# Cross-attention block with adaptive layer norms: half a score tile lowered by VectorE straight out of PSUM, two of four normalisations on GpSimd, one of four statistics on ScalarE, and a new order of the calls

## The chip, the core and the metric

The kernel runs on one core of one Trainium2 chip. The metric is the device time of one execution in microseconds (us), the median of several runs. One core has five engines that work side by side, each through its own queue of instructions in order: TensorE (PE in the profile; PEld is its weight load), VectorE (DVE), ScalarE (ACT), GpSimd (POOL) and SyncE (SP), which issues nearly all DMAs here.

## The reference

Everything is float32. There are 16 batches of 1024 query rows of 512 features, a context of 64 rows per batch, and 16 heads of 32 features.

```python
def _ada_ln(x, c, W_ss, b_ss):
    mu = jnp.mean(x, axis=-1, keepdims=True)
    var = jnp.mean((x - mu) ** 2, axis=-1, keepdims=True)
    h = (x - mu) / jnp.sqrt(var + EPS)
    ss = jax.nn.silu(c) @ W_ss + b_ss
    scale, bias = jnp.split(ss, 2, axis=-1)
    return (1.0 + scale)[:, None, :] * h + bias[:, None, :]
...
xq = _ada_ln(x_q, t_vec, Wss_q, bss_q)
xkv = _ada_ln(x_kv, t_vec, Wss_kv, bss_kv)
q = (xq @ Wq + bq).reshape(B, Lq, nh, dh)
kv = (xkv @ Wkv + bkv).reshape(B, Lkv, 2, nh, dh)
...
scores = jnp.einsum('bqhd,bkhd->bhqk', q, k) / jnp.sqrt(jnp.float32(dh))
attn = jax.nn.softmax(scores, axis=-1)
out = jnp.einsum('bhqk,bkhd->bqhd', attn, v).reshape(B, Lq, H)
return x_q + (out @ Wp + bp)
```

## The kernel before

The queries are cut into 32 blocks of 512 rows, numbered 0 to 31. The prologue computes the modulation, the keys K and the values V of all batches and starts the first blocks; a loop `for i in range(3, NB - 2)` (i from 3 to 29) is the steady state; a written-out tail finishes blocks 30 (`y`) and 31 (`z`). The steps of one block are spread over several turns of the loop, so that a turn works on six blocks at once: i, the two before it (`a = i - 1`, `b = i - 2`) and the ones after it.

The order of the instructions on every engine is the order in which the program calls the steps; no scheduler moves them. The tile framework adds the waits: an instruction waits for the last writer of what it reads, for the last readers of what it overwrites, and, where a PSUM tile is read by two engines, the later reader in program order waits for the earlier one.

The steps of one block that matter here, with the lines of the kernel before:

- `q_stats` (L286, L287): mean and variance of a block's rows, four parts t = 0 to 3 of 128 rows, on VectorE (BN_STATS and BN_AGGR). `q_scale` (L295 to L304) turns them into a scale and a shift on ScalarE and GpSimd. `hidden` (L327) normalises a part in place on ScalarE.
- `turn` (L357) transposes 32 by 32 on VectorE, `move` (L382) finishes the transposition with 16 DMAs, `scale_features` (L442) applies the modulation on ScalarE.
- The product with Wq is a seven-product scheme (Strassen): `query_product` n = 2 to 6, with the first and the seventh product split again by the same scheme into 4 and 3 quarter products (`quarter_products`, L605). GpSimd makes the sums of the operands (`feature_sums` L493, `feature_quarters` L581 to L583); ScalarE and VectorE read the results out of PSUM (`query_out`, `query_added`, `quarter_copies`, `quarter_adds`).
- `score_products(i, z)` (L738), z = 0 and 1 for the two halves of the 64 context rows: 16 small products that fill two PSUM tiles, `ps_i_z_0` and `ps_i_z_1` (half e = 0 and e = 1 of the score tile). There are only two such buffers (`ps_s`, `bufs=2`), shared by both halves z and by the result of `mix`. So `score_products(i, 1)` waits until both tiles of z = 0 have been read, and `mix` until both tiles of z = 1 have been.
- `maximum(i, z, e)` (L755) takes the column maxima of a PSUM tile on VectorE; `copied(i, z, e)` (L764) copies it to SBUF on ScalarE. Both read the same tile. `maxima` (L775, L784) joins the maxima of both halves and spreads them over a tile `mb`; `subtract` (L797) takes `mb` from each score half on GpSimd, in place in SBUF; `weights` (L808) is the exponential on ScalarE; `total` (L858) adds both halves on GpSimd, `row_total` (L863) sums the columns on VectorE, `inverse_rows` (L878) inverts them.
- `mix` (L936) multiplies by V, `divided` (L915) divides by the sums while it reads PSUM.
- The product with Wp is again a seven-product scheme, `product(i, n)` (L1086), with operand sums `row_sum` on GpSimd (L1051 to L1058). Its products accumulate in two PSUM banks, and `added(i, n)` (L1116) adds a finished product to the residual on VectorE.

In the loop before, each score half is read crosswise: VectorE begins with tile e = 0 while ScalarE copies e = 1, and then they change over.

## Time and profile before

| | |
|---|---|
| time, median of 3 runs | 997.28 us (996.85 to 998.1) |
| span of the profiled execution | 996.9 us |
| TensorE busy | 984.2 us (99%) |
| VectorE busy | 895.6 us (90%) |
| GpSimd busy | 895.4 us (90%) |
| ScalarE busy | 779.3 us (78%) |
| one turn of the loop (500.00 to 528.52) | 28.52 us |

The span runs from the first to the last instruction of the profiled execution; the median is 0.4 us above it. Busy times are sums of the records of an engine over the span. The end of a matmul's record is modelled, so TensorE is better read from the starts of its records. In the views below a row of the timeline holds start, duration, engine, line, operation, output<-input, number of records, and in brackets the idle time ahead of it and what ended it. Each float32 matmul of the program shows as two records.

### The profile page before, as it was taken

The page shows a single profiled execution, that of the slowest core. Times are in us where ns is not written, and L with a number is a line of the kernel's source. Part 1 is how long each engine was busy: PE and PEld are TensorE (multiplying, and loading weights), DVE is VectorE, ACT ScalarE, POOL GpSimd, SP SyncE. Part 2 cuts the span into 40 slices and gives each one's busy share as a digit, 9 for nine tenths or more (in the row PEclk, how much of TensorE's full clock was granted, in tenths as well). Part 3 has the DMA queues.
Part 4 walks back from the last instruction along what each step waited for, and adds up shares of the span by engine and source line. Part 5 has one row for each costly group of instructions (what it writes and reads, how often), then busy time and mean ns, then how long its engine had stood idle before and what let it go on. Part 6 is the DMA issues. An engine that isn't in the chain of part 4 may idle for free.

```text
span 996.9 us, 20564 instructions
## 1 busy us (share of the span) xinstructions
PE 984.2 (99%) x7465; PEld 760.7 (76%) x7465; DVE 895.6 (90%) x1318; ACT 779.3 (78%) x1165; POOL 895.4 (90%) x690
## 2 busy tenths in 40 slices
PE   7999999999999999999999999999999999999998
PEld 6878777787777877877778778777787787777756
DVE  7696899999999999999999999999999999987786
ACT  3878878888888888888888888888888888876620
POOL 2677899999999999999999999999999999999681
PEclk9999999999999999999999999999999999999999
DMA  9765655555655555566655555665555555544422
GB/s 308 264 165 151 156 164 156 140 165 180 190 181 176 159 165 152 151 182 186 183 176 152 173 145 155 185 188 178 176 150 175 151 154 182 148 132 130 145 85 97
DMA packets 115188, 165.77 MB, mean 166 GB/s; under 512 B 34920, under 2 KB 46464, under 8 KB 113168
## 3 DMA queue, kind: packets, MB, share of 16 engines
q1 hardware_dynamic: 114704, 163.93, 55.2%
q8 instruction: 59, 0.97, 0.4%
q0 software_dynamic: 384, 0.54, 0.2%
q14 instruction: 41, 0.34, 0.1%
HBM read 79.47 MB, written 34.60 MB: 114 GB/s over the span
## 4 chain that ended last, share of the span: by engine, by line
PE 88%; DMA 4%; DVE 3%; SPq 2%; POOL 1%; issue 1%; ACT 0%; DVEq 0%; POOLq 0%
PE pp L1086 36%; PE pq L534 27%; PE pq L605 10%; PE ps L738 6%; PE po L936 5%; PE pk_A L534 1%; PE pk_B L534 1%; DMA w_k_sb<-in_L_xcond_Wkv_dram 1%; DMA r<-in_x_dram 1%; PE pv_B L534 1%; DMA ltd<-lt 1%; DMA V_B<-stage_B 1%; DMA vr<-ltd 0%; POOL sum L858 0%; DVE l L826 0%
## 5 line engine op out<-in xcount | busy, mean ns | idle before, releaser
L797 POOL TENSOR_TENSOR s<-s,mb 128x2048 f32<-128x2048 f32 x64 | 290.6, 4564 | 20.3 <-DVE mb L784 13.4
L1086 PE MATMUL pp<-w_p_sb,ot 128*128 128x256 f32 x740 | 174.8, 379 | 1.1 <-DVE ot L915 1.1
L764 ACT COPY s<-ps 128x1024 f32<-128x1024 f32 x128 | 129.3, 1013 | 46.1 <-PE ps L738 34.0
L755 DVE TRANSPOSE_TENSOR_REDUCE m<-ps 128x32 f32<-128x1024 f32 x128 | 152.4, 1228 | 10.4 <-PE ps L738 9.3
L1086 PEld LDWEIGHTS pp<-w_p_sb,ot 128*128 128x128 f32 x740 | 138.2, 190 | 20.5 <-issue 2.8
L645 ACT ACTIVATE qt<-pq,bias_t 128x256 f32<-128x256 f32 x256 | 107.8, 475 | 48.8 <-PE pq L605 27.7
L858 POOL TENSOR_TENSOR sum<-s,p 128x2048 f32<-128x2048 f32 x30 | 136.5, 4549 | 1.6 <-ACT p L808 1.6
L1116 DVE TENSOR_TENSOR r<-pp,r 128x512 f32<-128x512 f32 x183 | 120.3, 669 | 13.8 <-ACT xt L442 6.8
L534 PE MATMUL pq<-xt,w_q_sums 128*128 128x256 f32 x512 | 123.8, 385 | 0.0
L534 PEld LDWEIGHTS pq<-xt,w_q_sums 128*128 128x128 f32 x512 | 95.0, 190 | 34.6 <-issue 22.6
L1086 PE MATMUL pp<-WT,ot 128*128 128x256 f32 x492 | 118.4, 383 | 0.0
L1086 PE MATMUL pp<-WT,s 128*128 128x256 f32 x488 | 116.1, 380 | 1.3 <-DVE r L1107 0.8
L817 ACT ACTIVATE s<-s 32x2048 f32<-32x2048 f32 x60 | 114.6, 1910 | 1.8 <-DMA p<-s 0.4
L1086 PEld LDWEIGHTS pp<-WT,ot 128*128 128x128 f32 x492 | 90.9, 190 | 19.1 <-issue 4.2
L1086 PEld LDWEIGHTS pp<-WT,s 128*128 128x128 f32 x488 | 88.2, 190 | 13.1 <-POOL s L1056 1.3
L327 ACT ACTIVATE x<-x,rstdq 128x512 f32<-128x512 f32 x128 | 94.8, 807 | 1.0 <-POOL rstdq L304 1.0
L442 ACT ACTIVATE xt<-xt,ss_q 128x512 f32<-128x512 f32 x124 | 94.0, 809 | 1.0 <-DMA xt<-ht 0.7
L915 DVE TENSOR_TENSOR ot<-po,vb 128x1024 f32<-128x1024 f32 x62 | 73.0, 1219 | 17.6 <-PE po L936 17.4
L286 DVE BATCH_NORM_STATS2 bs<-x 128x6 f32<-128x512 f32 x128 | 85.3, 666 | 0.0
L493 POOL TENSOR_TENSOR xt_sums<-xt 128x512 f32<-128x512 f32 x64 | 81.2, 1269 | 2.0 <-DMA x<-in_x_dram 1.3
L357 DVE STREAM_TRANSPOSE ht<-x 128x512 f32<-128x512 f32 x124 | 77.7, 679 | 4.7 <-DMA xt<-ht 2.2
L891 DVE STREAM_TRANSPOSE vb<-vr 128x2048 f32<-128x2048 f32 (+1 forms) x33 | 73.7, 2236 | 4.4 <-DMA vr<-ltd 4.4
(224 smaller groups left out, 1963.8 us busy)
## 6 DMA issues: line engine op xcount, KB each, us to landing
x<-in_x_dram SPq DMA_DIRECT2D x32, 1024.0 KB, 5.3
r<-in_x_dram SPq DMA_DIRECT2D x32, 1024.0 KB, 5.9
xt<-ht SPq DMA_DIRECT2D x488, 64.0 KB, 2.0
out_dram<-r SPq DMA_DIRECT2D x60, 512.0 KB, 4.7
p<-s SPq DMA_DIRECT2D x60, 256.0 KB, 3.8
wss_kv<-in_L_xcond_Wss_kv_dram SPq DMA_DIRECT2D x4, 512.0 KB, 7.2
wss_q<-in_L_xcond_Wss_q_dram SPq DMA_DIRECT2D x4, 512.0 KB, 11.0
vr<-ltd SPq DMA_DIRECT2D x128, 8.0 KB, 1.7
```

The lines of the kernel that those rows point to most:

```text
L327: nc.scalar.activation(dst, src, AF.Identity, bias=rstd[:, 1, j : j + 1], scale=rstd[:, 0, j : j + 1])
L442: nc.scalar.activation(xt[:, :, c, :], xt[:, :, c, :], AF.Identity, scale=ss["q"][:, c, b : b + 1], bias=ss["q"][:, NC + c, b : b + 1],)
L534: nc.tensor.matmul(out_, lhsT=lhsT, rhs=rhs, start=new and m == 0 and c == 0, stop=c == HC - 1, skip_group_check=True,)
L605: nc.tensor.matmul(qa["q", k][:, q * P : (q + 1) * P], lhsT=lhsT, rhs=rhs, start=first and q == 0, stop=True, skip_group_check=True,)
L645: nc.scalar.activation(dst, src, AF.Identity, bias=bq_t[:, o : o + 1])
L755: nc.vector.tensor_reduce(m_tiles[i][:, z, 2 * e : 2 * e + 2, :], s_banks[i, z][e].rearrange("p r (j a) -> p r j a", a=32), AX.X, ALU.max, ...
L764: nc.scalar.copy(s_tiles[i, z][:, 2 * e : 2 * e + 2, :], s_banks[i, z][e])
L797: eng.tensor_tensor(s_tiles[i, z], s_tiles[i, z], mb_tiles[i], ALU.subtract)
L817: nc.scalar.activation(s_tiles[i, 0][at + 32 : at + 64], raw_tiles[i][at : at + 32], AF.Exp, scale=SCALE)
L858: nc.gpsimd.tensor_tensor(t, s_tiles[i, 0], s_tiles[i, 1], ALU.add)
L1086: nc.tensor.matmul(to, lhsT=rows[:, c, t * P : (t + 1) * P], rhs=cols[:, c, :], start=n == 2 and (i, 2) not in seeded and t == 0 and c == ...
L1116: nc.vector.tensor_add(r, a, r)
```

## The change

In the loop:

- `copied(i, 1, 0)` (ScalarE) is gone. A new step `lowered(i, 0)` on VectorE reads the PSUM tile of z = 1, e = 0, subtracts `mb` and writes SBUF. The other half of z = 1 is still copied by ScalarE, and GpSimd subtracts on that half alone (`subtract_half`).
- Parts t = 0 and 1 of a block are normalised on GpSimd (`hidden_apart`), parts 2 and 3 as before on ScalarE.
- The statistics of part t = 0 are made on ScalarE (`q_stats_two`: two activations with a running sum, then a small GpSimd operation); parts 1 to 3 as before on VectorE.
- All calls of the prologue and of the loop stand in a new order. The loop's body is cut elsewhere: its first part, under `if i >= 4`, finishes the work of the turn before, and a written-out copy of it follows the loop. In the new order a turn begins `score_products(i, 0)`, `product(b, 6)`, `copied(i, 0, 0)`, `maximum(i, 0, 0)`, `maximum(i, 0, 1)`, `product(b, 7)`, the first quarter products, `copied(i, 0, 1)`, `added(b, 6)`, `score_products(i, 1)`.
- The small pools hold fewer buffers (`m2` 2 for 3, `lt` and `vr` 1 for 2). The tail after the loop is the same code, but for the part of Wp that is loaded again, which is now 512 KB instead of 256 KB.

Several new functions (`inner_*`, `exchanged`, `weights_whole`, `reciprocal_rows`, `read_rows`) are defined and never called.

```diff
+    def q_stats_two(i, ts, last=False):
...
+        for t in ts:
+            x = x_tiles[i][:, t, :]
+            junk = rpool.tile([P, HPC * TB], F32, tag="spread", name=f"squares_{i}_{t}")[:, :H]
+            nc.scalar.activation(junk, x, AF.Identity, scale=1.0 / H, accum_out=mv[:, t, 0:1])
+            nc.scalar.activation(
+                junk, x, AF.Square, scale=-1.0, bias=mv[:, t, 0:1], accum_out=mv[:, t, 1:2]
+            )
...
+    def hidden_apart(i, t):
+
+        row, rstd = x_tiles[i][:, t, :], q_rstd[i]
+        nc.gpsimd.tensor_scalar(
+            row, row, rstd[:, 0, t : t + 1], rstd[:, 1, t : t + 1], ALU.mult, ALU.add
+        )
...
+    def lowered(i, e):
+        rs = slice(2 * e, 2 * e + 2)
+        nc.vector.tensor_tensor(
+            s_tiles[i, 1][:, rs, :], s_banks[i, 1][e], mb_tiles[i][:, rs, :], ALU.subtract
+        )
+
+    def subtract_half(i, z, e):
+        rs = slice(2 * e, 2 * e + 2)
+        s = s_tiles[i, z][:, rs, :]
+        nc.gpsimd.tensor_tensor(s, s, mb_tiles[i][:, rs, :], ALU.subtract)
...
         score_products(i, 0)
...
+        product(b, 6)
...
+        copied(i, 0, 0)
...
         maximum(i, 0, 0)
...
+        maximum(i, 0, 1)
...
         quarter_products(n, 1, True)
-        product(b, 6)
         copied(i, 0, 1)
...
-        maximum(i, 0, 1)
         quarter_copies(n, 1)
-        copied(i, 0, 0)
...
```

The order is shown at three places, all at the beginning of the turn i = 15, in rows of operation, output<-inputs and size. `pq` is a query product, `pp` an output product, `ps_15_z_e` a score tile, `r` the residual, `lt` the row totals, `m2` the maxima.

TensorE before, ahead of `score_products(15, 0)`: query product 4, output product 2 of block 13, query product 3, output product 7, then the scores.

```order
L534 MATMUL pq_15_7_4623<-xt_sums_517,w_q_sb_101 128x256 x4
L1086 MATMUL pp_13_2_4711<-w_p_sb_104,ot_13_4686 128x256 x4
L534 MATMUL pq_15_1_4553<-xt_15_4192,w_q_sums_401 128x256 x4
L1086 MATMUL pp_13_3_4760<-WT_1338,ot_13_4686 128x256 x4
L738 MATMUL ps_15_0_0_4802<-qt_15_4614,K_A_130 32x512 x2
```

The same place on TensorE after the change.

```order
L1159 MATMUL pp_13_2_4690<-w_p_sb_104,ot_13_4688 128x256 x4
L558 MATMUL pq_15_1_4571<-xt_15_4219,w_q_sums_404 128x256 x4
L558 MATMUL pq_15_7_4647<-xt_sums_492,w_q_sb_101 128x256 x4
L1159 MATMUL pp_13_2_4734<-w_p_sb_104,ot_13_4688 128x256 x4
L762 MATMUL ps_15_0_0_4766<-qt_15_4644,K_A_130 32x512 x2
```

Output product 2 (`pp_13_2_4711` before, `pp_13_2_4734` after) has moved from three groups ahead of the scores to right in front of them, and output product 7 from ahead of the scores to between the two score halves.

VectorE before, around the maxima of the first score half.

```order
L1116 TENSOR_TENSOR r_13_4523<-pp_13_2_4711,r_13_4523 128x2x256
L652 TENSOR_TENSOR qt_15_4614<-pq_15_7_4623,qt_15_4614 128x2x4x32 x2
L863 TENSOR_REDUCE lt_14_4779<-sum_14_4722 128x64
L878 RECIPROCAL lt_14_4779<-lt_14_4779 128x64
L755 TENSOR_REDUCE m2_15_4820<-ps_15_0_0_4802 128x32
L755 TENSOR_REDUCE m2_15_4820<-ps_15_0_1_4803 128x32
```

The same place on VectorE after the change.

```order
L1292 TENSOR_TENSOR r_13_4471<-pp_13_2_4734,r_13_4471 128x2x256
L914 TENSOR_REDUCE lt_14_4803<-sum_14_4728 128x64
L779 TENSOR_REDUCE m2_15_4784<-ps_15_0_0_4766 128x32
L779 TENSOR_REDUCE m2_15_4784<-ps_15_0_1_4767 128x32
L929 RECIPROCAL lt_14_4803<-lt_14_4803 128x64
```

The row totals stand now directly between the addition of output product 2 and the two maxima.

ScalarE before, the copies of the first score half.

```order
L764 COPY s_15_0_4821<-ps_15_0_1_4803 128x1024
L616 COPY t_quarters_129<-pq_16_1_4823 128x256
L764 COPY s_15_0_4821<-ps_15_0_0_4802 128x1024
L817 ACTIVATE s_14_0_4551<-s_14_1_4584 32x2048
L546 COPY pq_16_2_4866<-pq_16_1_4823 128x512
```

The same place on ScalarE after the change.

```order
L788 COPY s_15_0_4785<-ps_15_0_0_4766 128x1024
L1104 COPY pp_13_3_4806<-b_diff_134 128x512
L296 ACTIVATE workq_4810<-mvq_18_4730,eps_sb_114 128x4
L297 ACTIVATE workq_4810<-workq_4810,ln_half_116 128x4
L299 ACTIVATE workq_4810<-workq_4810 128x4
L300 ACTIVATE workq_4810<-mvq_18_4730,eps_sb_114 128x4
L301 ACTIVATE workq_4810<-mvq_18_4730 128x4
L788 COPY s_15_0_4785<-ps_15_0_1_4767 128x1024
L640 COPY t_quarters_129<-pq_16_1_4842 128x256
```

Before, the copy of e = 1 comes first and waits for TensorE alone, and the copy of e = 0 waits for the maximum of e = 0. After, the copy of e = 0 comes first, both maxima follow on VectorE, and the copy of e = 1 waits for VectorE's maximum of e = 1.

More of the change, by code (lines that the diff above doesn't have):

```diff
@@ new lines, in cross_attention_block @@
+    q_scale(3)
+    context_product('B', 'k', 7)
+    query_out(1, 2)
+    move(2, ks=(0,))
+    move(2, ks=(1,))
+    query_product(1, 6)
+    copied(0, 1, 0)
+    hidden(3, (0,))
+    maximum(0, 1, 1)
+    hidden(3, (1,))
+    hidden(3, (3,))
+    query_out(1, 6)
+    load_x(4)
+    context_product('B', 'k', 6)
+    maximum(0, 1, 0)
+    move(2, ks=(2,))
+    query_product(1, 7)
+    context_out('B', 'k', 6)
+    query_product(1, 5)
+    maxima(0)
+    q_stats(4, (0,))
+    context_out('B', 'k', 7)
@@ new lines, in cross_attention_block @@
+    product(0, 2)
+    weights(1, 0)
+    query_out(2, 3)
+    query_added(2, 4)
+    nc.gpsimd.tensor_tensor(b_diff, b_second, b_first, ALU.subtract)
+    value_move('B', (1,))
+    score_products(2, 0)
+    hidden(4, (3,))
+    q_stats(5, (3,))
+    product(0, 1)
+    copied(2, 0, 1)
+    value_move('B', (3,))
+    turn(4, (1,))
+    turn(4, (2,))
+    copied(2, 0, 0)
+    turn(4, (3,))
+    total(1)
+    maximum(2, 0, 0)
+    maximum(2, 0, 1)
+    row_total(1)
+    query_product(3, 1)
+    load_x(6)
@@ L1505, in cross_attention_block @@
+    move(4, ks=(3,))
+    again(1, 1)
     weight_sums()
[L1506 to L1509 removed]
     maximum(2, 1, 0)
     maxima(2)
+    subtract(2, zs=(0,))
+    product(0, 6)
+    added(0, 6)
+    hidden(5, (3,))
     product(0, 7)
[L1513 to L1518 removed]
+    product(0, 5)
+    q_stats(6, (0,))
+    copied(2, 1, 0)
     added(0, 7)
     product(0, 4)
[L1521 removed]
@@ new lines, in cross_attention_block @@
+        if i >= 4:
+            hidden(f, (3,))
+        if i >= 4:
+            query_seed(i)
+        if i >= 4:
+            added(i - 3, 5)
+        if i >= 4:
+            product(i - 3, 4)
+        if i >= 4:
+            maxima(a)
+        if i >= 30:
+            load_residual(NB - 1)
+        if i >= 4:
+            query_product(i, 2)
+        if i >= 4:
+            again(b, 1)
+        if i >= 4:
+            turn(f, (0,))
+        if i >= 4:
+            copied(a, 1, 1)
+        if i >= 4:
+            lowered(a, 0)
@@ new lines, in cross_attention_block @@
+        if i >= 4:
+            turn(f, (3,))
+        if i >= 4:
+            total(a)
+        if i >= 4 and i <= 28:
+            q_stats_two(i + 3, (0,))
+        if i >= 4:
+            output_seed(b)
+        if i >= 4:
+            query_out(i, 3)
+        if i >= 4 and i <= 28:
+            q_stats(i + 3, (1,))
+        if i >= 4:
+            row_sum(b, 1)
+        if i >= 4:
+            load_residual(a)
+        if i >= 4:
+            product(b, 2)
+        if i >= 4 and i <= 28:
+            q_stats(i + 3, (2,))
@@ L1705, in cross_attention_block @@
-    y, z = NB - 2, NB - 1
+    product(27, 5)
+    quarter_products(30, 1, False)
+    maximum(29, 1, 1)
+    maximum(29, 1, 0)
+    feature_quarters(30, 7)
+    query_seed(30)
+    added(27, 5)
+    product(27, 4)
+    maxima(29)
+    load_residual(NB - 1)
+    query_product(30, 2)
+    again(28, 1)
+    copied(29, 1, 1)
+    lowered(29, 0)
+    product(27, 3)
+    query_out(30, 2)
+    quarter_products(30, 7, True)
+    quarter_copies(30, 7)
+    query_product(30, 6)
+    scale_features(31, (1,))
```

1106 lines of the change are left out of this document (623 added, 483 removed).

## The prediction

> **What bounds the kernel now.** I read the page first, then the chain of waits, then one turn of the loop stretch by stretch. The page's first part:
>
> ```profile
> PE 984.2 (99%) x7465; PEld 760.7 (76%) x7465; DVE 895.6 (90%) x1318; ACT 779.3 (78%) x1165; POOL 895.4 (90%) x690
> ```
>
> TensorE is busy in 99% of the span, but its ends are modelled, so the starts have to show whether it really never waits. The chain of the end, in order of time, gives the same piece of every turn:
>
> ```profile
> 501.22 3.45 PE pq L534 x16
> 505.56 3.46 PE pp L1086 x16
> 529.74 3.45 PE pq L534 x16
> ```
>
> One turn takes 529.74 - 501.22 = 28.52 us, and 16 records of 128x256 take 3.45 us, 0.216 us each. The window of one turn:
>
> ```profile
> 500.00:528.52 28.52, 28.52 (x222) 22.15 (x221) 26.95 (x41) 24.03 (x36) 27.53 (x22) 1.00 0.57 169
> ```
>
> The columns are the busy times of PE, PEld, DVE, ACT and POOL. The others have 1.0 to 4.5 us left in a turn. TensorE's timeline from 511.49 on:
>
> ```profile
> 510.50 1.06 PE L936 MATMUL po<-p,V_A 64*32 64x512 f32 x16
> 511.49 1.99 PE L534 MATMUL pq<-xt,w_q_sums 128*128 128x256 f32 x8
> 513.32 1.89 PE L1086 MATMUL pp<-w_p_sb,ot 128*128 128x256 f32 x8
> ...
> 516.78 1.89 PE L1086 MATMUL pp<-w_p_sb,ot 128*128 128x256 f32 x8
> ...
> 520.23 1.96 PE L1086 MATMUL pp<-WT,ot 128*128 128x256 f32 x8
> 522.11 1.14 PE L738 MATMUL ps<-qt,K_B 32*32 32x512 f32 x32
> 523.18 0.49 PE L605 MATMUL pq<-xt,w_q_sb 128*128 128x128 f32 x2
> 523.51 0.83 PE L605 MATMUL pq<-t_quarters,w_q_sb 128*128 128x128 f32 x6
> 524.18 1.89 PE L1086 MATMUL pp<-WT,s 128*128 128x256 f32 x8
> 526.00 1.14 PE L738 MATMUL ps<-qt,K_B 32*32 32x512 f32 x32
> ```
>
> From start to start a product of 8 records takes 1.73 us everywhere, 1.83 right behind the small-tile products (511.49 to 513.32), 1.82 to 1.88 ahead of them; 32 score records take 1.07. Nothing in this row of starts is a wait for another engine: the loop is TensorE's issue. The program of the changed kernel has the same matmuls in the same number, so the loop cannot fall below about 28.5 us a turn. What the change can win lies in the prologue (up to the first turn; 522.11 less 13 turns is 151 us) and the tail; what it can lose is any wait of TensorE that its new order brings into the turn.
>
> **The change part by part.** The durations are these groups (mean of one in ns behind the comma):
>
> ```profile
> L797 POOL TENSOR_TENSOR s<-s,mb 128x2048 f32<-128x2048 f32 x64 | 290.6, 4564 | 20.3 <-DVE mb L784 13.4 <-ACT qt L645 6.4 <-ACT s L764 0.4
> L1086 PE MATMUL pp<-w_p_sb,ot 128*128 128x256 f32 x740 | 174.8, 379 | 1.1 <-DVE ot L915 1.1
> L755 DVE TRANSPOSE_TENSOR_REDUCE m<-ps 128x32 f32<-128x1024 f32 x128 | 152.4, 1228 | 10.4 <-PE ps L738 9.3 <-issue 0.5
> L764 ACT COPY s<-ps 128x1024 f32<-128x1024 f32 x128 | 129.3, 1013 | 46.1 <-PE ps L738 34.0 <-DVE m L755 11.0
> L327 ACT ACTIVATE x<-x,rstdq 128x512 f32<-128x512 f32 x128 | 94.8, 807 | 1.0 <-POOL rstdq L304 1.0
> L915 DVE TENSOR_TENSOR ot<-po,vb 128x1024 f32<-128x1024 f32 x62 | 73.0, 1219 | 17.6 <-PE po L936 17.4
> L286 DVE BATCH_NORM_STATS2 bs<-x 128x6 f32<-128x512 f32 x128 | 85.3, 666 | 0.0
> L493 POOL TENSOR_TENSOR xt_sums<-xt 128x512 f32<-128x512 f32 x64 | 81.2, 1269 | 2.0 <-DMA x<-in_x_dram 1.3 <-ACT xt L431 0.4 <-issue 0.2
> L287 DVE BATCH_NORM_AGGREGATE mvq<-bs 128x2 f32<-128x6 f32 x128 | 23.3, 182 | 4.4
> L582 POOL TENSOR_TENSOR t_quarters<-xt,t_quarters 128x128 f32<-128x128 f32 x27 | 12.5, 463 | 2.1
> L302 POOL TENSOR_SCALAR workq<-workq 128x4 f32<-128x4 f32 x33 | 6.4, 194 | 2.9
> ```
>
> VectorE gains the lowering (as L915, 1.22 us, the same shape with one operand in PSUM) and loses one pair of statistics (0.67 + 0.18): 26.95 + 1.22 - 0.85 = 27.3 of 28.5 us. ScalarE loses one copy (1.01) and two normalisations (2 x 0.81) and gains two passes over 128x512, priced as L327 (0.81 each; the running sum is not in this trace, so up to twice that): 24.0 - 2.6 + 1.6 = 23.0, at most 24.6. GpSimd does half of one subtraction less: a 128x1024 one lies between 1.27 (128x512) and 4.56 us (128x2048), on the line 2.4, so it saves 2.2; a small operation adds 0.2 (as L302); two TENSOR_SCALAR over 128x512 are new. That shape is not in the trace. Above stands the two-input 128x512 with 1.27 us. Below stands the one large one-input operation:
>
> ```profile
> 1.02 0.29 POOL masks.py:199 TENSOR_SCALAR_AFFINE_SELECT ident<-ident 128x128 f32<-128x128 f32 x1
> ```
>
> The two-input operations take about 0.46 us for 128x128 (L582), so one input costs 0.63 of two; I take 0.63 x 1.27 = 0.80 us, from 0.62 (0.29 stretched by the slope from 128 elements, an estimate) to 1.27. GpSimd then has 27.53 - 2.2 + 0.2 + 1.6 = 27.1, at most 28.1. All three still fit under 28.5. The Trainium skill's page GPSIMD Engine Reference (Elementwise — side-by-side cycle accounting) speaks against the move: for elementwise work "use DVE for elementwise" stays its rule; its 512-element one-input loop takes 769 ns, and by that the sum would be 27.1 as well.
>
> So the amounts fit; what decides is the order at the beginning of a turn. I count from the start of output product 2, which now stands right ahead of the scores. TensorE without any wait: product 1.88 to the scores (as 520.23 to 522.11), scores 1.07, product 6 1.83, product 7 1.73, eight quarter records 1.00 less the 0.10 of the small tiles, 0.10 to change back, so 7.51 to the second score half, and 0.13 for the four records of its tile e = 0: **7.64 us** to the first record that needs the other buffer, e = 1.
>
> VectorE's and ScalarE's rows for the same chain:
>
> ```profile
> 511.65 2.36 DVE L915 TENSOR_TENSOR ot<-po,vb 128x1024 f32<-128x1024 f32 x2 [0.65 <-PE po L936]
> ...
> 518.76 0.69 DVE L1116 TENSOR_TENSOR r<-pp,r 128x512 f32<-128x512 f32 x1
> 519.37 0.74 DVE L652 TENSOR_TENSOR qt<-pq,qt 128x256 f32<-128x256 f32 x2
> 520.23 2.31 DVE L863 TRANSPOSE_TENSOR_REDUCE lt<-sum 128x64 f32<-128x2048 f32 x1
> 522.57 0.55 DVE L878 RECIPROCAL lt<-lt 128x64 f32<-128x64 f32 x1
> 523.45 2.38 DVE L755 TRANSPOSE_TENSOR_REDUCE m<-ps 128x32 f32<-128x1024 f32 x2 [0.32 <-PE ps L738]
> 525.75 0.25 DVE L622 TENSOR_TENSOR t_quarters<-pq,t_quarters 128x128 f32<-128x128 f32 x1
> ```
>
> ```profile
> 523.51 1.01 ACT L764 COPY s<-ps 128x1024 f32<-128x1024 f32 x1 [1.21 <-PE ps L738]
> ...
> 524.73 1.01 ACT L764 COPY s<-ps 128x1024 f32<-128x1024 f32 x1
> ```
>
> Before, the maximum of e = 0 and the copy of e = 1 run at once (523.45 and 523.51), then they change over: the copy of e = 0 starts at 524.73, 0.05 behind the end of its maximum (523.45 + 1.23), ends at 525.74, and TensorE starts the second half at 526.00. After the change they no longer cross: copy e = 0, maximum e = 0, maximum e = 1, copy e = 1, each behind the one before. The maxima also stand behind the row totals, and these behind the addition of output product 2:
>
> - the last of its 8 records starts 7 x 0.216 = 1.51 after the first and ends by its model at 1.89; VectorE follows 0.09 later (510.50 + 1.06 against 511.65): 1.98
> - addition 0.61 (518.76 to 519.37), row totals 2.34 (520.23 to 522.57): 4.93. The copy of e = 0 is done by 1.88 + 1.40 + 1.01 = 4.29 (522.11 to 523.51) and does not hold
> - maximum e = 0 1.15 (half of 523.45 to 525.75), maximum e = 1 1.23: 7.31
> - hand-over to ScalarE 0.05, copy of e = 1 1.01: 8.37
> - hand-over to TensorE at most 0.26 (525.74 to 526.00), at least 0.05 as to ScalarE; I take 0.15: **8.52 us**
>
> TensorE stands 8.52 - 7.64 = 0.88 us in every turn (0.78 to 0.99 by the hand-over). Behind the waiting matmul the whole of TensorE's queue stands, the next output product 2 with it, so the chain closes on itself and a turn takes 28.52 + 0.88 = **29.4 us**. The other engines have that much more slack: GpSimd's 27.1 to 28.1 and VectorE's 27.3 fit. One queue needs a look, SP's, where the swap of the score halves (`swapped`, before ahead of all sixteen `move` DMAs) now stands behind eight of them:
>
> ```profile
> 521.46 7.93 SPq L382 DMA_DIRECT2D xt<-ht  x12
> ```
>
> ```profile
> p<-s SPq DMA_DIRECT2D x60, 256.0 KB, 3.8
> ```
>
> A `move` takes 7.93 / 12 = 0.66 us to issue. The first waits for query product 3, which ends 1.73 before my zero; eight of them and two swaps end at -1.73 + 10 x 0.66 = 4.9, and the swap lands 3.8 later, at 8.7, where ScalarE's `again` has just come up behind the copy (8.37 + 0.38). TensorE needs ScalarE next some 4 us later, for the seed of query product 2, and `again` takes 1.9, so a swap that is 1 to 2 us late still costs nothing.
>
> Is the wait of the copy on the maximum needed? The rows alone can't say: 0.05 us behind the end of the maximum could be chance. The Trainium skill's page PSUM — Partial Sum Buffer (PSUM bank collisions raise a hardware error) says that two engines must not touch the same bank at once, two readers included. By that rule copy e = 1 cannot start ahead of its maximum's end and the turn is 29.4 us; without it, it would run with the row totals and the turn would stay at 28.52. This trace agrees: all copies of a turn lie outside the maximum of their own tile.
>
> The chain holds in the turns i = 4 to 29: 26 x 0.88 = 22.9 us. In turn i = 3 product 7 isn't between the halves (it is called in the prologue), so TensorE is there 1.73 earlier, while scores, copy, two maxima, copy follow each other: 1.40 + 1.01 + 1.15 + 1.23 + 0.05 + 1.01 + 0.15 = 6.00 after the scores' start against 1.07 + 1.83 + 0.90 + 0.10 + 0.13 = 4.03: **2.0 us**.
>
> The prologue has one clear wait:
>
> ```profile
> 15.80 2.02 PE L534 MATMUL pv_A<-w_v_sb,xk_A 128*128 128x256 f32 x8 [0.22 <-DVE xk_A L414]
> ...
> 19.24 3.69 PE L534 MATMUL pk_A<-xk_A,w_k_sb 128*128 128x256 f32 x16 [1.42 <-DMA w_k_sb<-in_L_xcond_Wkv_dram]
> ```
>
> The half of Wk that this product reads is now loaded ahead of the other half, and 1.4 us goes. TensorE's timeline is issued back to back from about 31 us on, so I take no more; a new wait among the reordered steps may eat it (from -3 to +1 us). The smaller pools, the peeled turn and the 256 KB more of Wp cost nothing that I can see: the loading lies beside the first half of the tail, whose code is the same. The 0.4 us between span and median stays.
>
> Sum against the span: 996.9 + 22.9 + 2.0 - 1.4 = 1020.4; with 0.4 to the median **1020.8 us**. With the ends of the hand-over (0.78 and 0.99), 0 to 2.5 for turn 3 and -3 to +1 for the prologue it is 1014.6 to 1026.5.
>
> **The rivals.** (1) Not slower: the second score buffer is free in time. Were the row totals and both maxima 0.9 us earlier (a hand-over at each step shorter than the rows show), the turn would stay at 28.52 and only the start would change. For it speaks that every amount fits and that the sum is close to the limit; against it that VectorE takes its instructions in order and the addition ahead of the row totals needs the last matmul before the scores. It decides at a chain below 7.64 us. Time: 997.3 - 1.4 = 995.9, from 994 to 998. (2) GpSimd becomes the bound: a TENSOR_SCALAR with two operands per partition could cost far more than one of two inputs. In a turn of 29.4 us it holds up to (29.4 - 25.5) / 2 = 1.9 us, or 1.6 with the 0.7 us that lie in GpSimd's 28.52 beside its records; at 2.0 us each the turn is 25.5 + 0.7 + 4.0 = 30.2, 26 x 1.7 = 44 us more: about 1041. Against it, both rows at hand lie below 1.3. (3) A part of the stall: the hand-overs are shorter and the maxima earlier, 0.4 a turn, about 1008.
>
> **How the numbers follow.** My forecast 0.72, (1) 0.13, (2) and other longer chains 0.09, (3) 0.06. The range 1007 to 1032 takes in the forecast's own 1014.6 to 1026.5, (3), and the lower part of (2). A measurement of this kernel tells 0.2% (2 us) from no change. Slower by more: 0.72 + 0.09 + 0.06 = 0.87; of (1), 0.08 are faster by more than 0.2% and 0.05 the same.
>
> **What would show it.** Right: the same piece of the chain repeats every 29.4 us; TensorE's second score half starts 0.9 us late in every turn, its releaser the ScalarE copy; that copy's releaser is the VectorE maximum; maxima, row totals and the copy enter the chain with some 6 us a turn. GpSimd's TENSOR_SCALAR 128x512 shows 0.6 to 1.3 us. The first key product starts near 17.5. Wrong: a turn of 28.5, or one that GpSimd fills without a gap, or a first score half that is read long before TensorE comes to the second.

## The result and the profile after

| | before | after |
|---|---|---|
| median of 4 runs each, same chip | 997.24 us | 1036.51 us (1035.29 to 1041.53) |
| ratio, 95% interval | 1 | 1.0399 (1.0375 to 1.0423) |
| span of the profiled execution | 996.9 us | 1035.0 us |
| one turn of the loop | 28.52 us | 29.29 us |

Two profiled executions lay far from the others of their kernel and are left out of all times and ratios: one of 4622 us of the kernel with ScalarE's order, and one of 1027.5 us, at a granted clock of 0.949, of the kernel with the Wk load alone.

The change costs 39 us. That is slower, as forecast, but 4.5 us above the upper end of the range. TensorE is busy for 98% of a longer span, with the same 7465 matmul records as before. That share alone hides what went wrong:

```profile
PE 1014.9 (98%) x7465; PEld 769.5 (74%) x7465; DVE 904.4 (87%) x1296; ACT 753.6 (73%) x1186; POOL 883.3 (85%) x767
```

The chain of waits in order of time, cut to the same place of two turns:

```profile
514.78 1.73 PE pp L1159 x8
516.51 1.07 PE ps L762 x32
...
522.24 1.79 PE ps L762 x32
...
544.07 1.73 PE pp L1159 x8
```

A turn takes 544.07 - 514.78 = 29.29 us. The two score halves are the same 32 records each, yet the first takes 1.07 and the second 1.79 us: 0.72 us of it is a wait inside the group, ahead of the records that need the buffer e = 1. The view names no releaser for so short a wait. In turn 3, where the same wait is longer, TensorE's timeline names one, ScalarE's copy:

```profile
169.48 1.05 PE L762 MATMUL ps<-qt,K_A 32*32 32x512 f32 x4
171.41 1.14 PE L762 MATMUL ps<-qt,K_A 32*32 32x512 f32 x28 [0.89 <-ACT s L788]
```

The three timelines of TensorE, VectorE and ScalarE show the chain as the prediction had it:

```profile
514.62 1.89 PE L1159 MATMUL pp<-w_p_sb,ot 128*128 128x256 f32 x8
...
522.17 1.86 PE L762 MATMUL ps<-qt,K_A 32*32 32x512 f32 x32
```

```profile
516.62 0.69 DVE L1292 TENSOR_TENSOR r<-pp,r 128x512 f32<-128x512 f32 x1 [0.22 <-PE pp L1159]
517.23 2.30 DVE L914 TRANSPOSE_TENSOR_REDUCE lt<-sum 128x64 f32<-128x2048 f32 x1
519.45 2.34 DVE L779 TRANSPOSE_TENSOR_REDUCE m<-ps 128x32 f32<-128x1024 f32 x2
```

```profile
517.74 1.02 ACT L788 COPY s<-ps 128x1024 f32<-128x1024 f32 x1 [1.28 <-PE ps L762]
...
521.82 1.01 ACT L788 COPY s<-ps 128x1024 f32<-128x1024 f32 x1 [1.51 <-DVE m L779]
```

Addition, row totals and both maxima follow each other without a gap from 516.62 to 521.79. The copy of e = 1 starts at 521.82 and ends at 522.83, 8.21 us behind the start of output product 2 (514.62); the prediction had 8.37.

The window of this turn (busy time of PE, PEld, DVE, ACT, POOL) and the groups of the new operations (busy us, mean ns of one):

```profile
500.00:529.29 29.29, 29.29 (x222) 22.32 (x221) 27.23 (x39) 23.13 (x37) 27.15 (x25) 1.00 0.58 165
```

```profile
L351 POOL TENSOR_SCALAR x<-x,rstdq 128x512 f32<-128x512 f32 x52 | 40.0, 769 | 2.7
L825 DVE TENSOR_TENSOR s<-ps,mb 128x1024 f32<-128x1024 f32 x27 | 32.0, 1186 | 0.1
L332 ACT ACTIVATE squares<-x,mvq 128x512 f32<-128x512 f32 x25 | 18.1, 724 | 0.8
L331 ACT ACTIVATE squares<-x 128x512 f32<-128x512 f32 x25 | 15.6, 623 | 0.0
L331 ACT ACTIVATION_READ_ACCUMULATOR squares<-x 128x1 f32 x25 | 4.9, 196 | 0.0
L332 ACT ACTIVATION_READ_ACCUMULATOR squares<-x,mvq 128x1 f32 x25 | 4.6, 185 | 0.0
```

The prices came out close: 0.77 us for the normalisation on GpSimd (0.80 taken), 1.19 for the lowering (1.22), 1.73 for the two passes on ScalarE with their running sums (1.6). So were the amounts of a turn: 27.2, 23.1 and 27.2 us (27.3, 23.0 and 27.1 taken).

**Where the 38 us of the span lie**, by TensorE's first start of each score group in both traces:

| stretch | before | after | difference |
|---|---|---|---|
| start, up to the loop's first scores | 151.24 | 165.60 | +14.4 |
| turn 3 | 28.51 | 28.66 | +0.15 |
| turns 4 to 28, 25 of them | 28.52 each | 29.29 each | +19.2 |
| turn 29 and the peeled copy behind the loop | 28.52 | 32.81 | +4.3 |
| from the scores of block 30 on | 75.5 | 75.7 | +0.2 |

The first scores of the loop, before and after:

```profile
151.24 1.14 PE L738 MATMUL ps<-qt,K_A 32*32 32x512 f32 x32
```

```profile
165.60 1.14 PE L762 MATMUL ps<-qt,K_A 32*32 32x512 f32 x32
```

The start is not equally long in every execution: three kernels of the experiments below that have this same start and other edits in the loop reach the loop's first scores at 162.9 to 163.7 us. Output product 7 of one block (1.73 us) now belongs to the peeled copy instead of turn 3. Without it turn 3 has +1.9 and the peeled copy +2.6. The largest miss is the start: it was to gain 1.4 us and lost 14.4. It contains several waits that the start before did not have. TensorE's and ScalarE's timelines at the very first scores, which came at 60.68 us before:

```profile
64.69 2.36 PE L762 MATMUL ps<-qt,K_A 32*32 32x512 f32 x32 [2.57 <-ACT qt L669]
```

```profile
63.46 0.81 ACT L466 ACTIVATE xt<-xt,ss_q 128x512 f32<-128x512 f32 x1 [4.65 <-DMA V_A<-stage_A]
64.18 0.82 ACT L669 ACTIVATE qt<-pq,bias_t 128x256 f32<-128x256 f32 x2
```

The scores wait for a query output that stands behind a scaling on ScalarE. The scaling reads `xt`, which the moves of block 1 write; the trace names another DMA that landed at the same time. In the program `load_x(3)`, 1 MB, is issued ahead of most of these moves. The DMA view of 44 to 66 us shows how late they land (KB each, median us from issue to landing):

```profile
xt<-ht SPq DMA_DIRECT2D x8, 64.0 KB, 7.3
xt<-ht POOLq DMA_DIRECT2D x8, 64.0 KB, 7.3
```

Over the whole kernel before, a move landed 2.0 us after its issue; the sixteen moves of block 1 took 4.4 (from SP's queue) and 2.8 us (from GpSimd's) there. In the changed kernel the load is issued at 52.03 us. The two of GpSimd's moves that were issued ahead of it landed after 2.2 us, the five behind it after 7.4 (medians of the DMA view in the windows 50.5 to 51.9 and 52.6 to 54.5). The same happens at 145 us, where the second residual load, also 1 MB, is issued ahead of the last moves of block 4:

```profile
153.71 6.77 PE L1159 MATMUL pp<-w_p_sb,ot 128*128 128x256 f32 x16 [3.20 <-ACT pp L1104]
```

```profile
152.36 0.81 ACT L466 ACTIVATE xt<-xt,ss_q 128x512 f32<-128x512 f32 x1 [3.87 <-DMA xt<-ht]
153.08 0.58 ACT L1104 COPY pp<-b_p_sb 128x512 f32<-128x512 f32 x1
```

At this second place 16 matmul records take 6.77 us in place of 3.45, so another 3.2 us are spent waiting inside it. I first took these two places, some 12 us together, for the cause of the whole loss in the start. The experiments did not bear that out.

In the peeled copy output product 7 directly follows output product 2 and waits for the bias copy into its bank (ACT pp L1104), which waits for the addition of product 2:

```profile
953.95 1.89 PE L1159 MATMUL pp<-w_p_sb,ot 128*128 128x256 f32 x8
957.39 1.97 PE L1159 MATMUL pp<-WT,ot 128*128 128x256 f32 x8 [1.55 <-ACT pp L1104]
```

### The profile page after: what moved, and what is told of

Read it like the earlier page. It is cut to its first block, busy times and chain, and to the rows that moved or that the text cites. A ratio compares the mean times of both kernels' runs of the same rounds, so it can differ in the third digit from the quotient of the medians.

```text
span 1035.0 us, 20853 instructions
## 1 busy us (share of the span) xinstructions
PE 1014.9 (98%) x7465; PEld 769.5 (74%) x7465; DVE 904.4 (87%) x1296; ACT 753.6 (73%) x1186; POOL 883.3 (85%) x767
## 4 chain that ended last, share of the span: by engine, by line
PE 83%; DVE 4%; DMA 4%; ACT 3%; POOL 2%; issue 2%; SPq 1%; ACTq 0%; DVEq 0%; POOLq 0%
PE pp L1159 35%; PE pq L558 25%; PE pq L629 9%; PE ps L762 8%; PE po L1009 5%; DMA xt<-ht 1%; DVE m L779 1%; POOL s L821 1%; DMA wss_kv<-in_L_xcond_Wss_kv_dram 1%; DMA ltd<-lt 1%; DMA p<-s 1%; ACT s L788 1%; ACT xt L466 1%; DMA vr<-ltd 0%; POOL wv_sums L491 0%
## 5 line engine op out<-in xcount | busy, mean ns | idle before, releaser
L821 POOL TENSOR_TENSOR s<-s,mb 128x2048 f32<-128x2048 f32 x37 | 168.9, 4568 | 18.7 <-DVE mb L808 18.3
L1159 PE MATMUL pp<-w_p_sb,ot 128*128 128x256 f32 x740 | 178.0, 385 | 4.6 <-ACT pp L1104 3.2
L788 ACT COPY s<-ps 128x1024 f32<-128x1024 f32 x101 | 101.8, 1012 | 94.6 <-DVE m L779 56.9
L1159 PEld LDWEIGHTS pp<-w_p_sb,ot 128*128 128x128 f32 x740 | 140.7, 193 | 24.9 <-ACT pp L1104 3.6
L1159 PE MATMUL pp<-WT,s 128*128 128x256 f32 x488 | 121.5, 392 | 0.9 <-DVE r L1283 0.8
L558 PE MATMUL pq<-xt,w_q_sums 128*128 128x256 f32 x512 | 121.3, 380 | 0.1
L676 DVE TENSOR_TENSOR qt<-pq,qt 128x256 f32<-128x256 f32 x128 | 48.3, 419 | 34.5 <-PE pq L558 33.6
L988 DVE TENSOR_TENSOR ot<-po,vb 128x1024 f32<-128x1024 f32 x62 | 73.0, 1218 | 4.4 <-PE po L1009 1.1
L808 DVE STREAM_TRANSPOSE mb<-m 128x2048 f32<-128x2048 f32 x32 | 74.0, 2311 | 1.1
```

The costliest lines, as they stand in the source:

```text
L558: nc.tensor.matmul(out_, lhsT=lhsT, rhs=rhs, start=new and m == 0 and c == 0, stop=c == HC - 1, skip_group_check=True,)
L788: nc.scalar.copy(s_tiles[i, z][:, 2 * e : 2 * e + 2, :], s_banks[i, z][e])
L821: eng.tensor_tensor(s_tiles[i, z], s_tiles[i, z], mb_tiles[i], ALU.subtract)
L1159: nc.tensor.matmul(to, lhsT=rows[:, c, t * P : (t + 1) * P], rhs=cols[:, c, :], start=n == 2 and (i, 2) not in seeded and t == 0 and c == ...
```

## The experiments

**The theories.** For the loop: the chain of addition, row totals, two maxima and copy holds TensorE (chain theory). Rival: the moved work makes GpSimd or VectorE the bound (amounts). For the start: two late transfers and ScalarE's order behind them. Rival: the loss is spread over the whole new order.

### The two copies crossed again

```diff
-        copied(i, 0, 0)
+        copied(i, 0, 1)
...
-        copied(i, 0, 1)
+        copied(i, 0, 0)
```

> The changed kernel with the copies of the first score half in the other order, as before the change: copy of e = 1 first, while the maximum of e = 0 is still to come; copy of e = 0 after that maximum. Chain theory: copy e = 0 starts behind the first maximum (520.6), not behind the second (521.79), and ends at 521.7, ahead of TensorE's second half (522.17); the stall of 0.77 a turn goes entirely, with the 1.9 of the first turn: 26 x 0.77 + 1.9 = 22 us less, about 1014.6, turn 28.5. Rival (amounts): 1036 as before.

Measured 1019.96 us (1015.85 to 1022.62), ratio 1.0216 (1.0186 to 1.0247). VectorE and ScalarE, and the window of one turn:

```profile
569.23 2.34 DVE L779 TRANSPOSE_TENSOR_REDUCE m<-ps 128x32 f32<-128x1024 f32 x2
```

```profile
570.48 1.01 ACT L788 COPY s<-ps 128x1024 f32<-128x1024 f32 x1 [0.32 <-DVE m L779]
```

```profile
566.22:594.85 28.63, 28.63 (x221) 22.14 (x220) 27.05 (x38) 23.23 (x37) 27.10 (x25) 1.00 0.56 168
```

The two maxima run from 569.23 to 571.57; the copy of e = 0 starts at 570.48, about 0.1 us behind the first of them, and the copy of e = 1 was done before. Most turns fall from 29.29 to 28.63 us (28.7 on average) with the same amounts: GpSimd still has 27.1 us. That refutes the amounts as the bound in this order and bears out the chain. The gain is 16.5 us of the 22 expected. Turn 3 gained nothing: its wait for the copy is gone, but it took 29.63 us in place of 28.66, now with waits for VectorE's lowering (L825) and division (L988). The other turns stay 0.11 us above 28.52. TensorE's starts show 0.10 of it: output product 7 starts 1.93 us after product 6 (567.29 and 569.22), where 1.83 was usual right behind small-tile products, and 0.14 us after the end of the bias copy into its bank (568.49 + 0.59). No run tried that copy by itself.

### The row totals behind the maxima

```diff
-            row_total(a)
...
         maximum(i, 0, 1)
+            row_total(a)
```

> The changed kernel with one line moved in the loop: the row totals of the tile before (2.30 us on VectorE) stand behind both maxima of the first score half, not ahead of them. Chain theory (row totals, two maxima, copy e = 1, second score half): the first maximum then waits only for the copy of its own tile, at 517.74 + 1.01 = 518.75 in the profiled turn, and the second ends at 521.1 in place of 521.79; the copy and TensorE follow 0.65 us earlier, 0.1 us of the 0.77 stay, a turn takes 28.6 us and the kernel 26 x 0.65 = 17 us less: about 1019.6. Rival (GpSimd's or VectorE's amount of work sets the turn): nothing is removed, so 1036 as before.

Measured 1051.92 us, ratio 1.0538 (1.0522 to 1.0554): 15 us slower, where 17 faster was expected. A turn takes 29.87 us. TensorE and VectorE:

```profile
526.39 1.23 PE L762 MATMUL ps<-qt,K_A 32*32 32x512 f32 x32
528.76 1.99 PE L1159 MATMUL pp<-WT,s 128*128 128x256 f32 x8 [1.14 <-DVE r L1292]
```

```profile
525.30 2.27 DVE L914 TRANSPOSE_TENSOR_REDUCE lt<-sum 128x64 f32<-128x2048 f32 x1
527.61 0.55 DVE L929 RECIPROCAL lt<-lt 128x64 f32<-128x64 f32 x1
528.08 0.63 DVE L1292 TENSOR_TENSOR r<-pp,r 128x512 f32<-128x512 f32 x1
```

The wait at the second score half is almost gone (1.23 us in place of 1.86), as the chain says. But row totals and reciprocal now stand ahead of addition 6, whose bank output product 5 needs right behind the scores, and TensorE waits there for 1.14 us. The chain was right and my sum was not: I had not asked who stands behind the new place. Between output product 2 and output product 5 VectorE has, in this order, no room for 2.3 us of work that is not urgent.

### The normalisations back on ScalarE

```diff
-            hidden_apart(f, 1)
+            hidden(f, (1,))
...
-            hidden_apart(i + 3, 0)
+            hidden(i + 3, (0,))
```

> The changed kernel with its order, but the two normalisations of a turn that went to GpSimd are back on ScalarE (0.81 us each) at the same places. GpSimd then has about 25.6 us a turn, ScalarE 24.7. Chain theory: GpSimd's share isn't on the chain; the turn stays near 29.3 and the time near 1036 (within 3 us, more if a normalisation falls between the copy of e = 0 and that of e = 1 on ScalarE, which adds up to 0.8 a turn, 1057 at most). Rival (GpSimd's new work, 27.15 us a turn, sets the turn): the turn falls to 28.5, about 1016.

Measured 1095.59 us, ratio 1.0983 (1.0967 to 1.1), far outside both expectations. TensorE, then ScalarE:

```profile
550.85 1.14 PE L762 MATMUL ps<-qt,K_A 32*32 32x512 f32 x28 [1.59 <-ACT s L788]
```

```profile
549.09 0.81 ACT L344 ACTIVATE x<-x,rstdq 128x512 f32<-128x512 f32 x1 [2.74 <-POOL rstdq L305]
549.81 0.99 ACT L788 COPY s<-ps 128x1024 f32<-128x1024 f32 x1
```

At this place the normalisation waits 2.74 us for its scale from GpSimd, and the copy of e = 1 waits behind it. So the run does not separate the theories; it adds a second late link to the chain. I had priced the moved instruction (0.81 us) and left out its operand. At this place on ScalarE the normalisation comes too early for its scale; a later place on ScalarE was not tried.

### The moved work alone, in the old order

```diff
-        copied(i, 1, 0)
         maxima(i)
+        lowered(i, 0)
...
-            hidden(i + 3, (1,))
+            hidden_apart(i + 3, 1)
...
-            hidden(i + 3, (0,))
+            hidden_apart(i + 3, 0)
...
-        subtract(i, zs=(1,))
+        subtract_half(i, 1, 1)
...
-            q_stats(i + 4, (2,))
+            q_stats_two(i + 4, (2,))
+            q_square_mean(i + 4, range(2, 3))
```

> The kernel before, its order and its start, with the moved work alone: one score tile lowered by VectorE out of PSUM, two normalisations of a turn on GpSimd, one of four statistics on ScalarE (the third of the four here). Theory that the amounts fit under TensorE's 28.52 us a turn and only the order costs: 996 to 999, no difference that can be told. Rival (the amounts or their dependences cost): a turn longer than 28.7 and 1003 or more.

This kernel and the next one also carry the changed kernel's smaller pools and its larger load of Wp. Measured 1027.29 us, ratio 1.0292 (1.0277 to 1.0306), a turn of 29.66 us: the rival's side. TensorE and VectorE show where:

```profile
518.48 1.99 PE L1159 MATMUL pp<-w_p_sb,ot 128*128 128x256 f32 x8 [0.29 <-DVE r L1292]
520.66 1.99 PE L1159 MATMUL pp<-WT,ot 128*128 128x256 f32 x8 [0.19 <-DVE r L1292]
```

```profile
516.60 1.23 DVE L825 TENSOR_TENSOR s<-ps,mb 128x1024 f32<-128x1024 f32 x1
517.74 0.68 DVE L1292 TENSOR_TENSOR r<-pp,r 128x512 f32<-128x512 f32 x1
```

The lowering stands ahead of addition 7, and TensorE waits for that addition and again for the next one. This leaves two readings, the amounts or the place. The next kernel tells them apart.

### The moved work alone, placed with care

Beside the edits of the last kernel: the lowering behind the quarter additions, the normalisations behind the subtractions, the statistics of part 1 instead of part 2 on ScalarE, and a bias ahead of two scalings.

```diff
         quarter_adds(n, 7)
+        lowered(i, 0)
...
+        subtract_half(i, 1, 1)
+            hidden_apart(i + 3, 1)
+            hidden_apart(i + 3, 0)
...
+            q_stats_two(i + 4, (1,))
+            q_square_mean(i + 4, range(1, 2))
...
+        added(a, 2)
+        biased(a, 3)
         scale_features(f, (0,))
```

> The kernel before with the three moved pieces of work, placed where nothing that TensorE waits for stands behind them: the lowering behind the quarter additions in place of ahead of output addition 7, both normalisations on GpSimd behind its subtractions, the statistics on ScalarE behind the sum of the weights, the bias of output product 7 ahead of two scalings. Theory that the amounts fit and a place ahead of an addition due for TensorE is what cost 1.1 us a turn: turns of 28.5 to 28.7, 997 to 1002. Rival (the amounts cost wherever they stand, engines being over 95% busy): turns of 29 or more, 1010 or more.

Measured 1002.55 us (1001.28 to 1005.37), ratio 1.0047 (1.0029 to 1.0065). Most turns take 28.69 us. A window of 28.60 us in the loop:

```profile
500.00:528.60 28.60, 28.60 (x236) 22.28 (x220) 27.37 (x39) 23.01 (x37) 26.65 (x24) 1.00 0.56 168
```

The amounts fit: with the same moved work the turn is 29.66 us in one place and 28.69 in another. Four steps were moved at once, so the share of each is not told apart. It is still 0.5% slower than the kernel before. The rows of TensorE's weight loads and of ScalarE show a wait that is left:

```profile
552.43 0.40 PEld L762 LDWEIGHTS ps<-qt,K_B 32*32 32x32 f32 x32 [0.33 <-ACT qt L669]
```

```profile
550.33 1.52 ACT L466 ACTIVATE xt<-xt,ss_q 128x512 f32<-128x512 f32 x2
551.75 0.81 ACT L669 ACTIVATE qt<-pq,bias_t 128x256 f32<-128x256 f32 x2
```

The first score half waits for a query output that stands behind two scalings. TensorE's next product starts at 553.67, so the 32 score records take 1.24 us in place of 1.07. These 0.17 us are all that the turn has above 28.52. That the moved work brings no gain fits the prediction's bound: TensorE's issue sets the turn, and relief of the other engines has nothing to win.

### The start of the kernel before

The changed loop and tail stand behind the 461 calls of the start in their old order.

```diff
-    load_x('A')
-    q_stats('A', (0,))
...
+    load_x("A")
+    load_scale_shift("kv", w_ss_kv, 0)
...
```

> The changed kernel's loop and tail behind the start (all that comes ahead of the loop) of the kernel before. Theory that the new order of the start itself costs 14.4 us: about 1022, the first scores of the loop at 151 to 152 us in place of 165.6, the turns unchanged at 29.3. Rival (the loop of the changed kernel enters with engines further behind, and takes the time back later): less than 7 us of gain, 1030 or more, with turns longer than 29.3 at the loop's beginning.

Measured 1022.39 us, ratio 1.0247 (1.0232 to 1.0262). The profiled execution reaches the loop's first scores at 150.05 us, 15.6 earlier; turn 3 then takes 30.11 us in place of 28.66, and the turns behind it stay at 29.29. The new order of the start costs 14.1 us by itself, and but for turn 3 the loop does not take them back.

### The big loads behind the moves, and ScalarE's order

```diff
-    load_x(3)
...
     move(1, two=True, ks=(3,))
+    load_x(3)
...
-    load_residual(1)
     move(4, ks=(3,))
+    load_residual(1)
```

> The changed kernel with two loads of 1 MB issued later in its start: the load of block 3 behind the four moves of tile 1, the second residual load behind the last move of tile 4. Theory of the late moves (a small transfer issued behind a 1 MB load lands 7 us after its issue in place of 2, ScalarE's scaling waits for it and TensorE for ScalarE): the two groups of stalls at 60 to 72 us (2.7 + 1.4 + 1.9) and at 150 to 160 us (3.4 + 3.1) go, 12.5 us at most, so 1024 to 1029. Rival (it is ScalarE's order, the scaling called ahead of what TensorE needs): the moves land 5 us earlier, but most of the stalls stay; 1032 or more.

```diff
-    scale_features(1, (3,))
...
     query_out(0, 3)
+    scale_features(1, (3,))
...
-    scale_features(4, (1,))
     biased(1, 2)
+    scale_features(4, (1,))
```

> The changed kernel with the loads as they are, but on ScalarE the scaling of features that waits for the late moves is called behind what TensorE waits for: behind the output of query product 3 of tile 0, and behind the bias of output product 1 of tile 1. Theory of the late moves: TensorE needs the scaled features itself right after (query product 1 of tile 1 at 67 us), so little is gained at the first place, and at most the 3.4 us wait on the bias at the second: 1032 to 1036. Rival (ScalarE's order alone): 6 to 12 us of gain, 1024 to 1030.

The kernel with both edits:

> The changed kernel with both small repairs of its start: the two 1 MB loads behind the moves, and ScalarE's scalings behind what TensorE waits for. If the late transfer and ScalarE's order are links of one chain: up to the 12.5 us of its two groups of stalls, 1024 to 1027. Rival (they only make room for the next waits, and the loss is spread): the sum of the single gains, 3.4 + 1.0, so 1032.

| | time | ratio, 95% interval |
|---|---|---|
| changed kernel | 1036.51 | 1.0399 (1.0375 to 1.0423) |
| loads behind | 1033.14 | 1.0346 (1.0322 to 1.037) |
| ScalarE's order | 1034.43 | 1.0373 (1.0356 to 1.0389) |
| both | 1031.71 | 1.0348 (1.0321 to 1.0375) |

With the loads behind, the moves land in time, as the DMA view of the same window shows, and the scaling on ScalarE follows without a wait:

```profile
xt<-ht POOLq DMA_DIRECT2D x8, 64.0 KB, 2.9
```

```profile
59.30 0.80 ACT L466 ACTIVATE xt<-xt,ss_q 128x512 f32<-128x512 f32 x1
```

In the kernel with both edits the same view gives 2.8 us for GpSimd's moves and 3.1 for SP's. So the mechanism of the late moves is shown: 7.3 us behind a 1 MB load, 2.9 ahead of it. The Trainium skill's page DMA: Bandwidth & Descriptors (Queues, rings and completion order) has each DMA engine take the descriptors of one queue in ring order, and the moves from SP agree with that. GpSimd's moves have a queue of their own in the DMA view and landed as late; what held them is not shown. But as a cause the late moves are worth 3 to 5 us of the time, known to some 3 us, and not 12. The loop's first scores do come earlier, at 159.53 us with the loads behind and at 158.55 with both edits (165.60 before these edits), but turn 3 then takes 31.1 us in place of 28.66. By TensorE's starts, waits of 1.9 and 2.0 us between 65 and 72 us and of 1.8 us at 149 us took the place of those that went (with the loads behind). ScalarE's order makes no difference that can be told, alone or on top.

### Where in the start the time goes

Four kernels cut the start at one point: one order's calls up to there, then the remaining calls in the other order. The first and second cut it at the first scores of tile 1, in either sense.

```diff
 (changed order up to)
     score_products(1, 0)
 (old order from there)
```

> The changed kernel with its start cut at the first scores of tile 1: the changed order ahead of that point, the order of the kernel before from there to the loop (the calls are the same in both). All old order gave 1022.4, all new 1036.5. If the loss lies where TensorE's starts fell behind, ahead of that point are some 6 of the 14 us (7.8 less 1.7 of work that is only moved): 1028 to 1030. Rival (the first half only hands the delay on, the second half takes it up): 1024 or less.

> The reverse: the old order up to the first scores of tile 1, the changed order from there to the loop. If the two halves add up: 1022.4 + 8 = 1030, with the late moves of tile 4 at about 140 us in it. Rival (the second half costs only because the first leaves ScalarE and VectorE behind): 1025 or less.

The third has the changed order up to `score_products(0, 0)`, the fourth from `score_products(2, 0)` on.

> The changed kernel with its start cut at the very first scores (tile 0): the changed order up to there, the old order from there to the loop. By TensorE's starts the changed kernel is 4.0 us late at that point, of which 1.7 are work that is only moved: 1022.4 + 2.3 = 1024.7. Of the 8.0 us of the first half 5.7 then lie between the first scores and those of tile 1. Rival (all of it stems from the stretch ahead of the first scores, as engines left behind): 1030.

> The old order up to the first scores of tile 2, the changed order from there to the loop. If the 5.8 us of the second half lie at the late moves of tile 4 (between 131 and 165 us, where the changed kernel lost 7 us): 1022.4 + 5 to 7 = 1027 to 1029. Rival (the loss of the second half lies between the scores of tile 1 and 2): 1024 or less.

| changed order in | time | ratio, 95% interval | above the old start |
|---|---|---|---|
| nothing (old start) | 1022.39 | 1.0247 (1.0232 to 1.0262) | 0 |
| up to scores of tile 0 | 1026.84 | 1.0291 (1.0274 to 1.0308) | 4.4 |
| up to scores of tile 1 | 1030.41 | 1.0322 (1.0303 to 1.0341) | 8.0 |
| from scores of tile 1 | 1028.24 | 1.03 (1.0281 to 1.0318) | 5.8 |
| from scores of tile 2 | 1027.18 | 1.0295 (1.0279 to 1.031) | 4.8 |
| everything | 1036.51 | 1.0399 (1.0375 to 1.0423) | 14.1 |

The halves add up: 8.0 + 5.8 = 13.8 of 14.1. By difference 4.4 us lie ahead of the first scores, 3.6 up to those of tile 1, about 1 up to tile 2, and 4.8 behind. The intervals reach 1.5 to 2.4 us to either side, so such a difference is known to 2 or 3 us, and the 1 can't be told from nothing. The loss is spread, and no single wait carries all of it.

### One load of the start alone, in the kernel before

```diff
-    load_context_weights(0, 1)
+    load_context_weights(0, 0)
...
-    load_context_weights(0, 0)
+    load_context_weights(0, 1)
```

> The kernel before with one thing of the change's start: the half of Wk that the first key product reads is loaded ahead of the other half. The prediction's term for the start (the wait of 1.4 us on that load goes): 996.5, 0.14% less, too little to tell from the time alone, so the trace decides: first key product at 17.5 in place of 19.24, and the first scores of the loop 1.4 us earlier. Rival (the next wait takes its place, as in the changed kernel, where TensorE then waited 1.5 us for VectorE's feature sums): the key product starts earlier, the loop does not.

Measured 997.54 us, ratio 0.9994 (0.9984 to 1.0004): no difference that can be told. Of its trace only the start of the key product is read:

```profile
17.98 3.76 PE L534 MATMUL pk_A<-xk_A,w_k_sb 128*128 128x256 f32 x16
```

The wait for Wk is gone (17.98 in place of 19.24). Three of the other kernels with the old order of the start have this product at 18.57 to 18.76, so the gain at this place is 0.6 to 1.3 us. Whether the 1.4 us reach the end, the time can't tell: its interval goes from 1.6 us less to 0.4 more. In the changed kernel the key product starts earlier still, and the next wait, for VectorE's sums, is as long as the one that went:

```profile
16.71 1.89 PE L558 MATMUL pk_A<-xk_A,w_k_sb 128*128 128x256 f32 x8
...
23.62 1.97 PE L558 MATMUL pk_A<-xk_sums_A,w_k_sums 128*128 128x256 f32 x8 [1.47 <-DVE xk_sums_A L517]
```

### All repairs together

Old start, crossed copies, and in the peeled copy output product 2 one product earlier:

```diff
+    product(28, 2)
     query_product(30, 4)
...
-    product(28, 2)
```

> The three repairs together: start of the kernel before, the two copies of the first score half in the old order in every turn, and in the peeled turn behind the loop output product 2 one product earlier, so that product 7, which needs its bank, does not follow it directly. If the terms add up: 1022.4 (old start) - 26 x 0.65 - 0.6 (the loop's first turn) - 1.7 (peeled turn) = 1003, turns of 28.64, so 0.5% above the kernel before: the moved work itself wins nothing, since TensorE's issue sets the turn, and 0.12 us a turn stay for more changes of the matmuls' tile size. A time below 996 would say that the moved work does win something.

Measured 1008.57 us, ratio 1.0113 (1.0097 to 1.013), 5 us above the sum. Most turns take 28.63 to 28.68 us, as expected. The repair of the peeled copy failed: turn 29 and the peeled copy took 32.97 us, where the kernel with only the copies crossed had 32.15. TensorE and ScalarE:

```profile
928.87 1.97 PE L1159 MATMUL pp<-WT,ot 128*128 128x256 f32 x8 [2.38 <-issue]
```

```profile
926.07 2.22 ACT L466 ACTIVATE xt<-xt,ss_q 128x512 f32<-128x512 f32 x3
928.18 0.59 ACT L1104 COPY pp<-b_diff 128x512 f32<-128x512 f32 x1
```

Product 2 is done in time now, but its addition on VectorE stands behind a query addition that waits 6.08 us for TensorE, and starts only at 927.21. The bias copy, which needs that addition and stands behind three scalings on ScalarE, starts at 928.18, and TensorE follows it, although its wait is listed as issue. That is 2.5 us more than the sum had here. Another 1.7 lie in turn 3, which is 31.19 us long and has waits for VectorE (the longest in the rows 1.35 us, for the lowering). No kernel beat the one before.

## Why the prediction was right or wrong

- **TensorE's issue bounds the loop: right.** Two orders of the moved work without long waits have turns of 28.63 and 28.69 us, none below 28.52.
- **The prices and the amounts: right**, the prices within 0.04 us each but for the two passes on ScalarE (1.73 for 1.6), the amounts of a turn within 0.13.
- **The chain at the beginning of the turn: right.** 0.72 us of wait in the record of the second score half and 0.77 us a turn, where 0.88 was forecast (0.78 to 0.99); the copy ended at 8.21 in place of 8.37. The crossed copies removed 0.66 a turn; of the other 0.11, 0.10 lie at the start of output product 7, whose cause was not tried. Of the signs that were named in advance one did not show: the chain of waits lists TensorE alone in these turns, without the maxima, row totals and copy; the wait lies inside a group of score records.
- **That the copy waits for the maximum of its tile: right as a wait**, but the rows don't show a rule of the chip at work. The framework orders two readers of one PSUM tile, and it is the order of the calls that decides which one waits; crossing them removed the stall.
- **Turn 3: right for this kernel, but the number does not carry over.** 2.0 us forecast, +1.9 measured, and the row names the copy. With the copies crossed this wait went, and turn 3 still had 2.8 us above its 26.79 us of work (28.52 less product 7), in waits for VectorE.
- **The failed step is the start**: "TensorE's timeline is issued back to back from about 31 us on, so I take no more; a new wait among the reordered steps may eat it (from -3 to +1 us)." It measured +14.4 in the trace (11.6 to 12.5 in three others with the same start) and 14.1 by exchange. Back-to-back starts before the change, with two waits of 0.26 and 0.24 us behind 31 us, show that the old order hides nearly every wait. They say nothing about a new order of 461 calls. The kernels with mixed starts show losses in nearly every part of it. Two late groups of moves give 3 to 5 us of them; which waits carry the other 9 or so is not settled. The wait on Wk went as forecast (first key product at 16.71 us, 17.5 forecast), and in the changed kernel a wait of 1.47 us for VectorE's sums followed it.
- **"The smaller pools, the peeled turn and the 256 KB more of Wp cost nothing that I can see": wrong for the peeled turn.** It has 2.6 us beside the moved product, 0.8 of it the loop's chain and most of the rest the wait of product 7 for its bank, 1.55 us in the row. The last stretch, with the Wp load, had only +0.2. The pools were not tried by themselves; the kernel with the moved work placed with care has them too, and its 0.17 us a turn are explained by another wait.
- **The sum.** With the start at +14.4 instead of -1.4 (15.8 more), 25 turns at 0.77 and the peeled copy at 2.6 instead of 26 turns at 0.88 (1.0 less), the 1020.8 become 1035.6; the span lay 0.4 us below the median before and 1.5 after, which gives the rest to 0.2 us.
- **The rivals.** "Not slower" failed. "GpSimd becomes the bound" failed: 0.77 us per normalisation, and the turn fell by 0.66 us with GpSimd's work unchanged. That its time of 1041 lies nearer to the result than the forecast does is chance. "A part of the stall" (0.4 us a turn) failed too: 0.77.

## What to carry to other kernels

When a change reorders code outside the loop, sum it with the same care as the loop: for each engine, look at what stands ahead of the steps that the bounding engine waits for, and on the DMA queues at big loads ahead of small transfers that someone waits for. An engine whose work fits in the turn can still stall the bounding one, since its queue is in order: with 1.2 us of lowering ahead of a due addition the turn took 29.66 us, with the lowering behind it (and three other steps moved) 28.69. When an instruction is moved, check two things beside its own price: when its operands come, and who stands behind its new place.
